# A two-layer sparse graph network on one core: order of the opening work, place of the order scatters, and the engines of the quantile mean

## The chip, the core and the metric

The kernel runs on one core of one Trainium2 chip. A core has a tensor engine (PE, with its weight loads counted apart as PEld), a vector engine (DVE), a scalar engine (ACT), GpSimd (POOL) and a sync engine (SP) that mostly issues transfers. Each engine works through its own list of instructions in order, and waits at an instruction until what it needs is there. The metric is the device time of one execution in microseconds.

## The reference

There are N = 4096 nodes with 128 features, and an adjacency matrix of 4096 x 4096 int32 with about 64 neighbours per node. Cut to what matters:

```python
# layer 0: graph attention, 8 heads
Wh = einsum('nd,hde->hne', nodes, W)
e  = leaky_relu((Wh @ a1)[:, :, None] + (Wh @ a2)[:, None, :])
att = softmax(where(adj > 0, e, -9e15))
h  = elu(einsum('hnm,hmd->hnd', att, Wh))
x1 = layernorm(nodes + elu(cat(h) @ W1 + b1))
# layer 1: mean of three quantiles over the kept neighbours
rank = cumsum(mask) - 1                     # every m-th neighbour is removed
keep = mask & ~((rank + 1) % m == 0)        # m = ceil(number / 2), if number > 5
svals = sort(where(keep, x1[None], big), axis=1)     # per feature
agg = sum(svals[ceil(q * n_keep) - 1] / 3 for q in (0.25, 0.5, 0.75))
out = (0.5 * agg + 0.5 * x1) @ W.T + b + x1
```

## The kernel before

Nodes are handled in 32 tiles of 128, one node per partition. `gnn` (L2138) runs layer 0 in `gat` (L761) and then, on a flag in memory, `sparse` (L1570) for graphs with few neighbours, the way taken here, or `general`, which takes no part in this execution.

**Lists of neighbours.** The class `Front` (L310) turns the adjacency matrix into sorted lists of neighbours, in six blocks of 4, 4, 6, 6, 6 and 6 tiles. `scan` (L360) loads quarters of rows (`a_i`, 512 KB, SP's queue), takes their sign on ACT (L371, L378: `nz`) and packs 16 columns into one number on PE (L380, `ps_words`, two buffers in PSUM). On DVE, `first` (L390) makes keys from the words (L393) and pulls out the largest eight in 13 rounds (`drain8`, L186 and L188: a maximum and a replacement); `second` (L398) unpacks the words in two more levels; `last_` (L736) sorts what was found. When all tiles of a block are through, `place` (L438) computes where each node's row goes (`pos_i`, L509, so that nodes with like counts share a tile), and POOL scatters the rows to memory (`rows_d`, L530). Then `keep` (L559) computes which neighbours layer 1 keeps, and at the end `order` (L619) and `scatter` (L668, 32 scatters of `order_d` on POOL) write the sequence of nodes for layer 1. `pieces` (L693) gives all this as a list of small steps; a call of `advance(n)` emits the next n of them, so the source chooses where between the attention's steps they are written.

**Attention.** `table` (L228) builds in memory `xf_d`, a row per node with its features and its eight terms of the attention: it loads x (`xf`), transposes it on PE (copies `xT_ta` on ACT, L143), multiplies the attention vectors (`abc_ta`) with the weights on DVE, projects on PE (`ps_fa`, L258), copies the result beside x on ACT (L259) and writes four transfers of 1024 rows (L261). All transfers of `table`, and the weight loads after it (L806 to L818), are issued on ACT's queue. For each of 64 half tiles, `load` (L873) then reads the lists back and gathers neighbour rows from `xf_d`, one row per partition and DMA (`nb`, L890, POOL, 2250 in all). DVE and ACT compute the attention's probabilities (L966, L974, L1005), PE sums weighted rows (L1012), and `combine` projects. The main loop (L1111) calls `advance(2)` per half tile.

**Layer 1.** In `sparse`, for each tile POOL gathers the kept neighbours' rows of x1 (`rows`, L1607, 2078 in all; three buffers). `compare` (L1632) is one step of a sorting network: ACT copies the low side to PSUM (`low`, L1645; small ones to SBUF, `low_s`), DVE takes the minimum (L1650) and the maximum (L1651); one-sided steps are L1653 and L1655. Steps of two tiles are interleaved. When a tile's steps are done, `quantile` (L1657) finds the rows that can be a node's quartile: for some late tiles a chain of minima and maxima (`cut`) first; then per quartile a weight (L1684: 1/3 where the position is the node's own, else 0), and DVE multiplies and adds row by row (L1695, L1698) into `agg`. `finish` (L1702), once per four tiles, has PE average with x1 (L1711, L1712), ACT copy (`comT`, L1716), PE apply the layer (L1722 to L1724), ACT copy `o` (L1728) and POOL scatter it (L1732). The parts of `finish` wait in a list, `waiting`, and are slipped into later comparisons: "copy" parts behind the comparison's own ACT copy, "bank" parts for PE in the last bank of the comparison's PSUM tile, ahead of its minimum:

```python
nc.scalar.copy(packed, lows)
if waiting and waiting[0][0] == "copy":
    waiting.pop(0)[1]()
elif waiting and SMALL < k <= PAIRS - FOUR:
    waiting.pop(0)[1](t[:, (PAIRS - FOUR) * D :])
nc.vector.tensor_tensor(lows, packed, highs, op=ALU.min)
nc.vector.tensor_tensor(highs, packed, highs, op=ALU.max)
```

**What sets the order.** The source is written in one sequence, but the framework arranges each engine's list itself, by data dependencies and its own estimates of when operands are ready; `issue_after(i)` binds what is emitted under it behind instruction i. Buffers of a pool bind too: a tile may be written only when the earlier use of its memory is over.

Of the kernel before, what the change touches and what calls it, by code (L numbers as in the profile page):

```python
# [50 lines left out]
P = 128  # L51
N = 4096
D = 128
# [37 lines left out]
FOUR = 4  # L91

# [135 lines left out]
def table(tc, nc, c, x, w, a1, a2, xf_d):  # L228

    with tc.tile_pool(name="ta", bufs=1) as tp, tc.tile_pool(  # L230
        name="ta_ps", bufs=2, space=PSUM
    ) as psum:
        w_sb = tp.tile([P, H, D], F32, name="w_ta")
        nc.scalar.dma_start(out=w_sb, in_=w.rearrange("h d e -> d h e"))
        pad = tp.tile([1, XF], F32, name="pad_x")
        nc.gpsimd.memset(pad, 0.0)
        nc.gpsimd.memset(pad[:, D : D + H], -BIG)
        nc.scalar.dma_start(out=xf_d[0:1, :], in_=pad)
        xf = tp.tile([P, NT, XF], F32, name="xf")
        for i in range(4):  # L240
            nc.scalar.dma_start(
                out=xf[:, ts(i, 8), :D],
                in_=x[ts(i, 1024), :].rearrange("(t p) d -> p t d", p=P),
            )
        xT = tp.tile([P, N], F32, name="xT_ta")
        transpose_all(nc, psum, xT, [xf[:, t, :D] for t in range(NT)], c["idf"])
        wa = tp.tile([P, 2 * H], F32, name="wa_ta")
        for i, a in enumerate((a2, a1)):
            abc = tp.tile([P, H, D], F32, name="abc_ta", bufs=2)
            nc.scalar.dma_start(  # L250
                out=abc.rearrange("p h e -> p (h e)"),
                in_=a.rearrange("h e -> (h e)").partition_broadcast(P),
            )
            nc.vector.tensor_mul(abc, abc, w_sb)
            nc.vector.reduce_sum(wa[:, ts(i, H)], abc, axis=AX.X)
        ps_f = psum.tile([P, NT, 2 * H], F32, name="ps_fa", bufs=1)
        for t in range(NT):
            nc.tensor.matmul(ps_f[:, t, :], xT[:, ts(t, P)], wa, start=True, stop=True)  # L258
        nc.scalar.copy(xf[:, :, D:], ps_f)  # L259
        for i in range(4):  # L260
            nc.scalar.dma_start(  # L261
                out=xf_d[1 + i * 1024 : 1 + (i + 1) * 1024, :].rearrange(
                    "(t p) d -> p t d", p=P
                ),
                in_=xf[:, ts(i, 8), :],
            )
# [43 lines left out]
class Front:  # L310
# [3 lines left out]
    def __init__(self, tc, nc, c, adj, meta_d, ctx):  # L314
# [43 lines left out]
        self.words, self.lists, self.counts = {}, {}, {}  # L358

# [78 lines left out]
    def place(self, b):  # L438
# [70 lines left out]
        nc.vector.tensor_copy(pos_i, pos)  # L509
# [183 lines left out]
    def pieces(self, order_d, flag_d):  # L693
# [10 lines left out]
        for b, n in enumerate(BLOCKS):  # L704
            lists = self.tp.tile([P, max(BLOCKS), C1], F32, name="lists")

            def open_(b=b, lists=lists):
                self.lists[b] = lists

            out.append(("open", open_))  # L710
            at = START[b]
            while at < START[b] + n:
                m = min(BATCH, START[b] + n - at)
                if n % BATCH:
                    m = n // -(-n // BATCH)
                bufs = {}

                def start(bufs=bufs):
                    bufs["k1"] = self.one.tile([P, BATCH, C1], F32, name="k1")
                    bufs["cand"] = self.one.tile([P, BATCH, CAND], F32, name="cand")  # L720

                for j in range(m):

                    def one_(t=at + j, j=j, bufs=bufs, start=start):
                        if j == 0:
                            start()
                        ahead(t)
                        self.first(t, bufs["k1"][:, j, :])

                    out.append((None, one_))  # L730
                out.append(
                    (None, lambda t=at, m=m, bufs=bufs: self.second(t, m, bufs["k1"], bufs["cand"]))
                )
                for j in range(m):

                    def last_(t=at + j, j=j, b=b, bufs=bufs):  # L736
                        to = self.lists[b][:, t - START[b], :]
                        drain8(self.nc, to, bufs["cand"][:, j, :], C1 // 8, -1.0e6)
                        self.nc.vector.tensor_scalar(
                            self.spill[:, t, 4:5], to[:, C1 - 1 :], 0.0, None, op0=ALU.is_ge  # L740
                        )

                    out.append((None, last_))
                at += m
            out.append((b, lambda b=b: self.place(b)))
            if b:
                out.append((None, lambda b=b: self.keep(b - 1)))
# [8 lines left out]
        for t in range(NT):  # L756
            out.append((None, lambda t=t: self.scatter(t, state["pos"], order_d)))
        return out


def gat(tc, nc, c, x, adj, xf_d, meta_d, order_d, flag_d, w, a1, a2, w1, b1, gamma, beta, x1_d):  # L761
# [22 lines left out]
    with ExitStack() as ctx:  # L784
        front = Front(tc, nc, c, adj, meta_d, ctx)
        todo = front.pieces(order_d, flag_d)
# [13 lines left out]
        table(tc, nc, c, x, w, a1, a2, xf_d)  # L800
# [5 lines left out]
        nc.scalar.dma_start(out=w_sb, in_=w.rearrange("h d e -> d h e"))  # L806
        w1_sb = one.tile([P, H, D], F32, name="w1_ga")
        nc.scalar.dma_start(out=w1_sb, in_=w1.rearrange("(h e) o -> e h o", e=D))
        b1_sb = one.tile([P, 1], F32, name="b1_ga")
        nc.scalar.dma_start(out=b1_sb, in_=b1.rearrange("(o k) -> o k", k=1))  # L810
        bc = {}
        for name, src in (("gamma", gamma), ("beta", beta)):
            bc[name] = one.tile([P, D], F32, name=f"{name}_ga")
            nc.scalar.dma_start(out=bc[name], in_=src.partition_broadcast(P))
        for row, value in PADS:
            pad = one.tile([1, D], F32, name="pad", bufs=2)
            nc.vector.memset(pad, value)
            nc.scalar.dma_start(out=x1_d[row : row + 1, :], in_=pad)  # L818
# [292 lines left out]
        for u in range(2 * NT):  # L1111
            t, half = divmod(u, 2)
            if u + 3 < 2 * NT:
                held[u + 3] = load(u + 3)
            if not half and t + 1 < NT:
# [454 lines left out]
def sparse(tc, nc, c, x1_d, meta_d, order_d, w, b, out):  # L1570


    with tc.tile_pool(name="sp1", bufs=1) as one, tc.tile_pool(
# [11 lines left out]
        nc.scalar.mul(half, c["idf"], 0.5)  # L1585
        wT = one.tile([P, D], F32, name="lwT")
# [4 lines left out]
        third = float(np.float32(1.0 / NQ))  # L1591
# [65 lines left out]
        def quantile(t, rows, info, extra, agg):  # L1657

            shift = MIDDLE - HIGH[t] // 2
            for q, (lo, hi) in enumerate(places(t)):  # L1660
                n = hi - lo + 1
                if extra:
                    cut = one.tile([P, 3 * (80 - MAIN) * D], F32, name="cut")
                    grid = view(cut, 0, (extra, n), (1, extra))
                    nc.vector.tensor_tensor(
                        grid,
                        view(rows, lo - extra - 1, (1, n), (1, extra)),
                        view(rows, MAIN, (0, n), (1, extra)),
# [3 lines left out]
                    while m > 1:  # L1672
                        h = m // 2
                        a = view(cut, 0, (extra, n), (1, h))
                        nc.vector.tensor_tensor(
                            a, a, view(cut, m - h, (extra, n), (1, h)), op=ALU.min
                        )
                        m -= h
                    best = view(rows, lo - 1, (1, n))
                    nc.vector.tensor_tensor(best, best, view(cut, 0, (extra, n)), op=ALU.min)  # L1680
                if q == 0:
                    begun = False
                weight = tp.tile([P, 8], F32, name="weight", bufs=4)
                nc.vector.tensor_scalar(  # L1684
                    weight[:, :n],
                    iota_p[:, lo + shift : hi + 1 + shift],
                    info.bitcast(F32)[:, POS + q : POS + q + 1],
                    third,
                    op0=ALU.is_equal,
                    op1=ALU.mult,  # L1690
                )
                for i in range(n):
                    v = view(rows, lo - 1 + i)
                    if not begun:
                        nc.vector.tensor_scalar(agg, v, weight[:, i : i + 1], None, op0=ALU.mult)  # L1695
                        begun = True
                    else:
                        nc.vector.scalar_tensor_tensor(  # L1698
                            agg, v, weight[:, i : i + 1], agg, op0=ALU.mult, op1=ALU.add
                        )  # L1700

        def finish(xs, agg, infos):  # L1702
# [3 lines left out]

            def halves_(ps):
                made["ps"] = ps
                for j in range(m):
                    com = ps[:, ts(j, P)]  # L1710
                    nc.tensor.matmul(com, agg[:, j, :], half, start=True, stop=False)  # L1711
                    nc.tensor.matmul(com, xs[:, j, :], half, start=False, stop=True)  # L1712

            def half_copy():
                made["comT"] = one.tile([P, FOUR * P], F32, name="comT")
                nc.scalar.copy(made["comT"][:, : m * P], made["ps"][:, : m * P])  # L1716

            def layer(ps):
                made["ps"] = ps
                for j in range(m):  # L1720
# [3 lines left out]
                    nc.tensor.matmul(to, made["comT"][:, ts(j, P)], wT, start=False, stop=True)  # L1724
# [14 lines left out]
            return [("bank", halves_), ("copy", half_copy), ("bank", layer), ("copy", layer_copy)]  # L1739
# [3 lines left out]
        def load(t):  # L1743
            rows = three.tile([P, max(HIGH), D], F32, name="rows")
            first, _ = ENDS[t]
            if t == first:
                group[first] = (
                    tp.tile([P, FOUR, D], F32, name="xs"),
                    tp.tile([P, FOUR, D], F32, name="agg"),
# [17 lines left out]
        for t in range(NT + 1):  # L1767
# [9 lines left out]
            if t > 0:  # L1777
                first, n = ENDS[t - 1]
                agg = group[first][1]
                quantile(t - 1, *held.pop(t - 1), plans[t - 1][2], agg[:, t - 1 - first, :])  # L1780
# [411 lines left out]
```

## Time and profile before

| | |
|---|---|
| median of the runs | 7742.63 us (7739.8 to 7743.64, 3 runs) |
| the profiled execution | 7742.94 us |
| its span, first to last instruction | 7741.1 us |
| DVE busy | 5841.9 us (75%) |
| POOL busy | 4386.7 us (57%) |
| ACT busy | 2162.5 us (28%) |
| PE busy | 1051.4 us (14%) |

A profile line names a source line, an engine, an operation and its operands (out<-in), a count, the busy time and the mean duration, and the idle time of the engine just before, with what ended it. "issue" is idle time for which the profile shows no wait. In the page's slices each digit is the busy share in tenths of one fortieth of the span (193.5 us). A line of waits reads: who waited, for whom, microseconds in all, times, and the longest. A window's line gives the stretch, its length, each engine's busy time with the number of instructions, the granted tensor clock, the share of the DMA engines and GB/s.

### The profile page before, as it was taken

The page shows a single profiled execution, that of the slowest core. Times are in us where ns is not written, and L with a number is a line of the kernel's source. Part 1 is how long each engine was busy: PE and PEld are TensorE (multiplying, and loading weights), DVE is VectorE, ACT ScalarE, POOL GpSimd, SP SyncE. Part 2 cuts the span into 40 slices and gives each one's busy share as a digit, 9 for nine tenths or more (in the row PEclk, how much of TensorE's full clock was granted, in tenths as well). Part 3 has the DMA queues.
Part 4 walks back from the last instruction along what each step waited for, and adds up shares of the span by engine and source line. Part 5 has one row for each costly group of instructions (what it writes and reads, how often), then busy time and mean ns, then how long its engine had stood idle before and what let it go on. Part 6 is the DMA issues. An engine that isn't in the chain of part 4 may idle for free. (4 is left out here: it accounts for less than half of the span.)

```text
span 7741.1 us, 30455 instructions
## 1 busy us (share of the span) xinstructions
PE 1051.4 (14%) x5811; PEld 887.8 (11%) x5811; DVE 5841.9 (75%) x9358; ACT 2162.5 (28%) x2127; POOL 4386.7 (57%) x4564
## 2 busy tenths in 40 slices
PE   3233242332232223200000000000000000000000
PEld 1122232222232222100000000000000000000000
DVE  6456465564332222289999999999999999999999
ACT  5021112000000000133333333333333333333332
POOL 0777777777777777575545636354635534554400
PEclk5566666665566666655555555555555555555555
DMA  5232324222222222111111101011101101111100
GB/s 183 67 100 78 97 78 113 64 60 56 47 56 56 56 56 56 41 48 37 35 32 36 42 24 43 27 38 31 45 23 36 36 27 29 37 36 31 31 3 1
DMA packets 222435, 385.05 MB, mean 50 GB/s; under 512 B 121622, under 2 KB 133274, under 8 KB 222234
## 3 DMA queue, kind: packets, MB, share of 16 engines
q0 software_dynamic: 145664, 305.55, 15.4%
q1 hardware_dynamic: 64258, 70.19, 3.0%
q10 hardware_dynamic: 12312, 7.28, 0.3%
q14 instruction: 154, 1.26, 0.1%
q8 instruction: 47, 0.77, 0.0%
HBM read 372.41 MB, written 10.31 MB: 49 GB/s over the span
## 5 line engine op out<-in xcount | busy, mean ns | idle before, releaser
L1607 POOL DMA_INDIRECT rows<-x_d,info x2078 | 2022.4, 973 | 1962.4 <-DVE agg L1698 1272.7
L890 POOL DMA_INDIRECT nb<-xf_d,ids x2250 | 2140.2, 951 | 697.0 <-issue 652.8
L1645 ACT COPY low<-rows 128x2048 f32<-128x2048 f32 (+8 forms) x1022 | 1561.3, 1533 | 2599.7 <-DVE rows L1651 1964.0
L1650 DVE TENSOR_TENSOR rows<-low,rows 128x2048 f32<-128x2048 f32 (+8 forms) x1022 | 1883.1, 1861 | 114.5 <-ACT low L1645 33.8
L1651 DVE TENSOR_TENSOR rows<-low,rows 128x2048 f32<-128x2048 f32 (+8 forms) x1022 | 1881.7, 1860 | 4.7
L966 DVE TENSOR_TENSOR e<-nb,ps_small 128x144 f32<-128x144 f32 (+8 forms) x166 | 43.5, 264 | 1314.1 <-DMA nb<-xf_d,ids 1246.9
L1012 PE MATMUL ps_z<-spread,nb 128*128 128x128 f32 x4500 | 612.1, 304 | 770.2 <-DVE spread L1005 749.0
L1012 PEld LDWEIGHTS ps_z<-spread,nb 128*128 128x128 f32 x4500 | 601.0, 219 | 804.5 <-DVE spread L1005 367.3
L1711 PE MATMUL low<-half_i,agg 128*128 128x128 f32 x64 | 22.2, 451 | 4297.1 <-ACT low L1645 4191.2
L974 ACT ACTIVATE ps_e<-e 128x256 f32<-128x256 f32 (+4 forms) x64 | 26.1, 408 | 1941.1 <-DVE e L966 1856.6
L1711 PEld LDWEIGHTS low<-half_i,agg 128*128 128x128 f32 x64 | 16.9, 325 | 4300.6 <-ACT low L1645 4193.6
L1005 DVE TENSOR_TENSOR spread<-e,ps_small 128x1152 f32<-128x1152 f32 (+4 forms) x312 | 342.9, 1107 | 87.8 <-PE ps_z L1012 85.3
L1732 POOL DMA_INDIRECT out<-o,info x32 | 33.4, 1044 | 383.6 <-ACT o L1728 359.3
L371 ACT ACTIVATE nz<-a_i 128x1024 bf16<-128x1024 int32 x128 | 134.4, 1051 | 229.4 <-DMA a_i<-in_adj 188.5
L1645 ACT COPY low_s<-rows 128x512 f32<-128x512 f32 (+3 forms) x325 | 139.8, 471 | 142.8 <-DVE rows L1650 61.4
L186 DVE MAX8 k<-key 128x8 f32<-128x256 f32 x416 | 165.7, 413 | 0.9
L1650 DVE TENSOR_TENSOR rows<-low_s,rows 128x512 f32<-128x512 f32 (+3 forms) x325 | 158.0, 499 | 2.6 <-ACT low_s L1645 2.1
L1651 DVE TENSOR_TENSOR rows<-low_s,rows 128x512 f32<-128x512 f32 (+3 forms) x325 | 158.7, 499 | 0.3
L188 DVE MATCH_REPLACE8 key<-k,key 128x256 f32<-128x256 f32 x384 | 155.9, 408 | 0.0
L904 DVE TENSOR_TENSOR mine<-me,group 128x64 f32<-128x64 f32 x32 | 6.8, 213 | 196.6 <-DMA me<-xf_d,info 193.5
L380 PE MATMUL ps_words<-nz,pows 128*128 128x512 bf16 (+1 forms) x272 | 109.8, 559 | 291.9 <-ACT nz L378 192.8
L1653 DVE TENSOR_TENSOR rows<-rows 128x256 f32<-128x256 f32 (+8 forms) x245 | 141.4, 579 | 0.2
(227 smaller groups left out, 2584.8 us busy)
## 6 DMA issues: line engine op xcount, KB each, us to landing
a_i<-in_adj SPq DMA_DIRECT2D x128, 512.0 KB, 4.4
nb<-xf_d,ids POOLq DMA_INDIRECT x2250, 2.5
rows<-x_d,info POOLq DMA_INDIRECT x2078, 2.4
xf_d<-xf ACTq DMA_DIRECT2D x4, 576.0 KB
xf<-in_x ACTq DMA_DIRECT2D x4, 512.0 KB
meta_d<-rowdata_k SPq DMA_DIRECT2D x4, 324.0 KB, 4.0
abc_ta<-in_L_gnn_a ACTq DMA_DIRECT2D x2, 512.0 KB, 8.6
w_ga<-in_L_gnn_W ACTq DMA_DIRECT2D x2, 512.0 KB, 4.9
```

The lines of the kernel that those rows point to most:

```text
L186: nc.vector.max(out=top, in_=work)
L188: nc.vector.match_replace(out=work, in_to_replace=top, in_values=work, imm_value=gone)
L371: nc.scalar.activation(nz[:, j, :], a_i, AF.Relu, scale=-1.0, accum_out=self.negative[:, k : k + 1],)
L380: nc.tensor.matmul(ps_w[:, :m, :], self.pows[:, 4 * i + b, :], nz[:, :m, ts(b, NG1)], start=i + b == 0, stop=i + b == 6,)
L890: gather = nc.gpsimd.indirect_dma_start(out=rows[:, at + i, :], out_offset=None, in_=xf_d, in_offset=bass.IndirectOffsetOnAxis(ap=ids[:, k ...
L1005: last = nc.vector.tensor_tensor(spread[:, :m], e[:, at : at + m, :].unsqueeze(2).to_broadcast(shape), own.unsqueeze(1).unsqueeze(3).to_br ...
L1012: product = nc.tensor.matmul(ps_z[:, g, :], rows[:, k + i0 + i, :D], spread[:, i].rearrange("p j h -> p (j h)"), start=i0 + i == 0, stop=i ...
L1607: nc.gpsimd.indirect_dma_start(out=row, out_offset=None, in_=x1_d, in_offset=bass.IndirectOffsetOnAxis(ap=info[:, col : col + 1], axis=0),)
L1645: nc.scalar.copy(packed, lows)
L1650: nc.vector.tensor_tensor(lows, packed, highs, op=ALU.min)
L1651: nc.vector.tensor_tensor(highs, packed, highs, op=ALU.max)
L1653: nc.vector.tensor_tensor(lows, lows, highs, op=ALU.min)
```

## The change

It has three parts. (A) The transfers of `table` and the weight loads go to POOL's queue; the scans of block 0 are emitted within `table` (`between`), ahead of the transposes; and `first` of the later blocks may be issued only behind block 0's `pos_i`. (B) The 32 order scatters are taken out of the list of pieces and emitted once no further half tile is left to load. (C) The quantile mean no longer runs on DVE: DVE makes one weight (1 or 0) for all three quartiles of a tile, ACT multiplies each found row by it (`picked`), and PE adds the rows and x1 by products with scaled identities (`sixth`, `half`), per tile; ACT copies the sum. The chain of minima and maxima is done in pieces of at most 32 rows.

```diff
-def table(tc, nc, c, x, w, a1, a2, xf_d):
+def table(tc, nc, c, x, w, a1, a2, xf_d, between):
...
-        nc.scalar.dma_start(out=w_sb, in_=w.rearrange("h d e -> d h e"))
+        nc.gpsimd.dma_start(out=w_sb, in_=w.rearrange("h d e -> d h e"))
...
+        for a in (a2, a1):
+            abc = tp.tile([P, H, D], F32, name="abc_ta", bufs=2)
+            nc.gpsimd.dma_start(
...
         for i in range(4):
-            nc.scalar.dma_start(
+            nc.gpsimd.dma_start(
                 out=xf[:, ts(i, 8), :D],
...
+        between()
+        for i, abc in enumerate(abcs):
+            nc.vector.tensor_mul(abc, abc, w_sb)
+            nc.vector.reduce_sum(wa[:, ts(i, H)], abc, axis=AX.X)
...
         for i in range(4):
-            nc.scalar.dma_start(
+            nc.gpsimd.dma_start(
                 out=xf_d[1 + i * 1024 : 1 + (i + 1) * 1024, :].rearrange(
...
-        nc.vector.tensor_copy(pos_i, pos)
+        placed = nc.vector.tensor_copy(pos_i, pos)
+        if b == 0:
+            self.placed = placed.ins
...
-                        self.first(t, bufs["k1"][:, j, :])
+                        with ExitStack() as order:
+                            if self.placed is not None:
+                                order.enter_context(self.tc.issue_after(self.placed))
+                            self.first(t, bufs["k1"][:, j, :])
...
-        for t in range(NT):
-            out.append((None, lambda t=t: self.scatter(t, state["pos"], order_d)))
-        return out
+        late = [lambda t=t: self.scatter(t, state["pos"], order_d) for t in range(NT)]
+        return out, late
...
         advance(1)
-        table(tc, nc, c, x, w, a1, a2, xf_d)
+        table(tc, nc, c, x, w, a1, a2, xf_d, lambda: advance(2))
...
-        nc.scalar.dma_start(out=w_sb, in_=w.rearrange("h d e -> d h e"))
+        nc.gpsimd.dma_start(out=w_sb, in_=w.rearrange("h d e -> d h e"))
...
                 held[u + 3] = load(u + 3)
+            elif late:
+                advance(len(todo))
+                for piece in late:
+                    piece()
+                late = []
...
+        sixth = one.tile([P, P], F32, name="sixth_i")
+        nc.scalar.mul(sixth, c["idf"], 0.5 * float(np.float32(1.0 / NQ)))
...
+            nc.vector.tensor_tensor(
+                weight[:, :, : last - first + 1],
+                iota_p[:, first + shift : last + 1 + shift].unsqueeze(1).to_broadcast(shape),
+                info.bitcast(F32)[:, POS : POS + NQ].unsqueeze(2).to_broadcast(shape),
+                op=ALU.is_equal,
+            )
...
                 for i in range(n):
-                    v = view(rows, lo - 1 + i)
-                    if not begun:
-                        nc.vector.tensor_scalar(agg, v, weight[:, i : i + 1], None, op0=ALU.mult)
-                        begun = True
-                    else:
-                        nc.vector.scalar_tensor_tensor(
-                            agg, v, weight[:, i : i + 1], agg, op0=ALU.mult, op1=ALU.add
-                        )
+                    at = lo - first + i
+                    found.append((view(rows, lo - 1 + i), weight[:, q, at : at + 1]))
+            return found
+
+        def pick(found, x1, comT):
+            made = {}
+            def scale():
+                made["v"] = tp.tile([P, MOST, D], F32, name="picked", bufs=1)
+                for i, (v, weight) in enumerate(found):
+                    nc.scalar.mul(made["v"][:, i, :], v, weight)
+            def sums(ps):
+                made["ps"] = ps[:, :P]
+                for i in range(len(found)):
+                    nc.tensor.matmul(
+                        made["ps"], made["v"][:, i, :], sixth, start=i == 0, stop=False
+                    )
+                nc.tensor.matmul(made["ps"], x1, half, start=False, stop=True)
+            return [
+                ("copy", scale),
+                ("bank", sums),
+                ("copy", lambda: nc.scalar.copy(comT, made["ps"])),
+            ]
...
-            return [("bank", halves_), ("copy", half_copy), ("bank", layer), ("copy", layer_copy)]
+            return [("bank", layer), ("copy", layer_copy)]
...
+                found = quantile(t - 1, *held.pop(t - 1), plans[t - 1][2])
+                waiting += pick(found, xs[:, at, :], comT[:, at, :])
```

## The prediction

> **What bounds the kernel now.** The slices of the page come first: they show stages with different limits. In slice 0 POOL does nothing; to about slice 16 it is the busy engine; from slice 17 VectorE (DVE) is at nine tenths.
>
> ```profile
> DVE  6456465564332222289999999999999999999999
> ACT  5021112000000000133333333333333333333332
> POOL 0777777777777777575545636354635534554400
> ```
>
> Cut at the stages, busy time per engine (columns: PE, PE weight loads, DVE, ACT, POOL) says how full each is.
>
> ```profile
> 0.00:170.50 170.50, 58.37 (x194) 32.77 (x194) 114.75 (x595) 102.28 (x160) 1.59 (x11) 0.57 0.58 187
> 170.50:3189.00 3018.50, 872.82 (x5154) 758.93 (x5154) 1342.87 (x5088) 345.14 (x578) 2260.52 (x2374) 0.63 0.28 69
> 3245.00:7741.10 4496.10, 94.53 (x320) 74.34 (x320) 4354.56 (x3599) 1702.05 (x1365) 2120.43 (x2174) 0.50 0.11 32
> ```
>
> In the first stage no engine is full: it is a chain that ends at DVE's `pos_i`, for which POOL waits 166.6 us. In the second, POOL goes from gather to gather, 951 ns and 0.30 us of issue, 1.25 us each, while DVE waits 1246.9 us for `nb`. In the third DVE has 4354.6 of 4496.1 us, so a microsecond of DVE work there is a microsecond of time. Groups of the page and of the third stage:
>
> ```profile
> L890 POOL DMA_INDIRECT nb<-xf_d,ids x2250 | 2140.2, 951 | 697.0 <-issue 652.8
> ...
> L1698 DVE SCALAR_TENSOR_TENSOR agg<-rows,weight,agg 128x128 f32<-128x128 f32 x118 | 40.2, 341 | 0.8
> ...
> L1645 ACT COPY low_s<-rows 128x128 f32<-128x128 f32 x57 | 16.3, 294 | 12.3 <-DVE rows L1655 5.8 <-DVE rows L1650 4.2 <-DVE rows L1651 1.8
> ```
>
> The waits of the first 200 us tell what delays `pos_i`:
>
> ```profile
> POOL rows_d L530 <- DVE pos_i L509: 166.6, 1, 166.6
> ...
> DVE pad L817 <- DMA xf_d<-xf: 22.0, 1, 22.0
> ...
> ACT xf L259 <- PE ps_fa L258: 14.7, 1, 14.7
> ...
> ACT nz L378 <- DMA w_ga<-in_L_gnn_W: 10.2, 1, 10.2
> ...
> ACT nz L378 <- issue: 4.1, 1, 4.1
> ```
>
> ACT stands still three times (14.7, 4.1 and 10.2 us) in the table's copy and DMA issues, with adjacency scans queued behind; DVE then gets the words of tiles 2 and 3 at 87.9 us.
>
> **Part A: first block ahead of the table.** Nineteen DMAs leave ACT's queue for POOL's; block 0's scans stand before the table, and DVE's first-level searches of later blocks are held behind block 0's `pos_i`.
>
> The ACT side: sixteen quarter-row scans are all that tiles 0 to 3 need, 2.31 us each (four took 9.22 us from 78.88). From a start near 6 us: 6 + 16 x 2.31 + 3.3 (`pows`) + 8 x 0.53 (`xT` copies) = 50.5, and about 3.5 for late loads and the last words on PE: words of the pair at about 54 us (50 to 60) instead of 87.4.
>
> The DVE side: after 7 of the 13 rounds of the pair's search stands a memset that waits until the `xf_d` writes have landed (the same wait is the 22.0 us of L817 now). DVE is there at about 66. The copy into `xf` follows the seventeenth scan on ACT, at about 59. Now the writes go out on ACT, 48.43 us, and are down at 61.6, 13.1 later. On POOL no row shows a plain DMA of 1024 rows. The nearest are indirect ones: 0.95 us for 128 descriptors. From below, one plain DMA costs as much as one of those (landed about 72, DVE not held long); from above, eight times as much, 7.6 us (landed about 92). Neither is nearer; I take the middle, 4.3: landed 79, so a wait of 13 us stays.
>
> Then, with durations of the trace: 0.9 (memset and small ones) + 8.6 (six rounds left) + 13.5 (second level) + 28 (last level, 27.9 now) + 11.5 (placing, with `keep` between) = 62.5; `pos_i` at 141.5 instead of 170.1. What drops out on the way is 17.8 us of later blocks' key work, which comes after `pos_i` and fills DVE's waits for gathers (about 104 us idle between 200 and 400). From `pos_i` to the first gather is 9.85 us now (170.08 to 179.93), kept: 151.4 against 179.9, **-28.5**. POOL's issue carries this through the second stage one to one, if no later block's `pos_i` is late: block 1 has it at 369.7 for a scatter at 432.9, block 4 at 1524.1 for one at 1540.3. DVE had waited for gathers before each, so these times move with POOL. Ends: -36 by the low price, -16 by the high one, -12 with late words too.
>
> A rule speaks against this part. The Trainium skill, "DMA: Bandwidth & Descriptors", section "SWDGE vs HWDGE vs iDMA", gives plain transfers to SP or ACT, because GpSimd builds descriptors in software. By the rule alone A loses: the landing goes from 61.6 to 79 or 92. By the rows it wins: ACT's three stalls, 29 us, are on the path, POOL is idle 166.6 us, and the later landing runs into a DVE that is itself busy until 66. I follow the rows for the sign, and the rule for the 13 us that stay.
>
> **Part B: order scatters last.** The 32 scatters of `order_d` (1965.8 to 2081 us, 32 x 1.25 = 40 us of POOL) are written after the last gather in the source. But in the compiled order of POOL's instructions they stand among the gathers as before: 13 behind the last block's rows, then 6, 8, 4, 1, with some 180 gathers still to come. No instruction moves, so **0**; if they did move, into POOL's idle time at the end of the stage, -40.
>
> **Part C: quantile mean.** Removed from DVE: L1698 118 times (40.2 us), and by rows of the same view L1695 32 times (8.8) and L1684 96 times (20.1): 69.1 us busy. Records overlap by 0.07 us, as here (start, duration):
>
> ```profile
> 7719.01 0.28 DVE L1653 TENSOR_TENSOR rows<-rows 128x128 f32<-128x128 f32 x1
> 7719.22 0.74 DVE L1655 TENSOR_TENSOR rows<-rows 128x256 f32<-128x256 f32 x2
> ```
>
> 69.1 - 246 x 0.07 = 51.9. Added: 32 weight comparisons at the 277 ns of a 128x128 operation, 0.21 net each, 6.6; six more cut operations in one tile, 1.2. DVE: **-44**. The last tile's 13 (4.99 us) give way to 14 scales and 15 matmuls at the very end, 4 to 7 us: no gain there, within 2 either way.
>
> ACT gets 150 scales of 128x128. No row has a scale by a per-partition pointer; nearest are the plain copy at 294 ns and `yT`, whose bias pointer costs 55 ns over its twin without (471 against 416). About 0.30 us net each, 4.7 per tile: 1.4 us. ACT is 38% busy there and mostly waits for DVE, but DVE now waits 33.8 us in 43 places for ACT's copy, so the lead is short at times: estimated a quarter of a microsecond per tile, **+8** (0 to 45).
>
> PE gets 3 to 7 matmuls per tile (15 for tiles 0 and 31) in place of 8 per four tiles. They use the last bank of a `low` tile, and the minimum behind waits:
>
> ```profile
> DVE rows L1650 <- ACT low L1645: 33.8, 43, 1.9
> ...
> DVE rows L1650 <- PE low L1724: 22.1, 7, 5.5
> ...
> DVE rows L1650 <- PE low L1712: 2.5, 4, 1.3
> ```
>
> The twelve matmuls of the layer stall DVE 3.2 us a time, the eight of the halves 0.6. Five (0.43 each, 2.2 us) should nearly hide: 0.2 x 32 = **+6** (0 to 70), less the 2.5 of the halves. POOL's gathers wait for the freeing of `rows` with at least 22 us to spare. C: -44 - 2.5 + 6 + 8 = **-32.5** (-46 to +69 with both ends at once).
>
> Here a rule bears too: "ScalarE: Activation LUTs", section "Rules for kernel authors", puts multiplication on VectorE, not ScalarE. Per operation that agrees with the trace (277 against 294 ns). By the rule the move costs 150 x 0.02 = 3 us; by the stage rows it frees 44, since DVE is full and ACT idle.
>
> **Sum.** -28.5 + 0 - 32.5 = -61 on the profiled 7742.94 (span 7741.1, 1.8 around it). The median of the runs shown is 7742.63, 0.3 lower: 7742.6 - 61 = 7681.6, said as **7680**. What a measurement can tell is 0.2%, 15.5 us.
>
> **Rivals.** (1) A turns into a wait for POOL's descriptors: x and the weights also go through POOL, so `xf` itself is late, and DVE stands at the pad memset till 92 or beyond. For: no plain DMA on POOL in the trace, the rule above. Against: POOL has nothing else. A gives -16 to 0: 7694 to 7710. (2) C is eaten, ending on the other side. In a comparison with a sum, ACT copy, PE matmuls and DVE minimum stand in a row; if scales (1.4) and sums (2.2) both show fully, 3.6 x 32 = 115, C is +69; with A: 7742.6 - 28.5 + 69 = 7783. For: the layer's 3.2 us. Against: the halves' 0.6. It is slower from 2.3 us per tile on, (28.5 + 46.5) / 32. (3) C is half eaten, 1.1 us per tile (35), -11: 7703. (4) B happens after all: 7640. A and C both leading to nothing is left among (2) and (3).
>
> **How the numbers follow.** Likeliest (A and C as summed) 0.57, own range 7660 to 7697; rival 1 0.20; rival 3 0.13; rival 4 0.06; rival 2 0.04. The range reaches from 7648 (low price for A, C unhindered, without B) to 7716 (rivals 1 and 3 in part together), leaving out some 0.2. Faster by over 0.2% means below 7727: all but rival 2 and a sliver of 1 with 3, 0.93; same 0.03; slower 0.04.
>
> **What would show it.** A: `pos_i` near 141 and first gather near 151; DVE's pad wait 5 to 26 us; no ACT stall on `w_ga`; words of tiles 2 and 3 near 54. B: order scatters still between 1900 and 2100. C: DVE busy in the third stage 44 lower; waits of L1650's successor for ACT under 45, for PE under 32. Wrong: `pos_i` after 155, a wait for `pos_i` at a later block, or PE and ACT waits of over 60 together.

## The result

The changed kernel takes 7694.65 us (median of 4 runs, 7692.66 to 7695.29), the kernel before 7741.75 (7739.8 to 7743.64): a ratio of 0.9939, 95% interval 0.9922 to 0.9956, or 47 us less. The prediction was 7680, 62 us less, with a range of 7648 to 7716. The profiled execution has a span of 7693.5 us against 7741.1, 47.6 us less. Some runs below, marked as paused, were taken while the chip added pauses, mostly of 10 to 45 us, to every kernel, so that the kernel before took 8506 or 8553 us; their times are compared only with those of the kernel before taken beside them, and otherwise their traces are read by their waits.

Of the changed kernel, the windows of the front up to `pos_i` and the first gather, the stage of gathers, the passage to layer 1, layer 1, and the end (stretch, length, busy time of PE, PE weight loads, DVE, ACT, POOL):

```profile
132.60:142.30 9.70, 4.81 (x12) 1.64 (x13) 9.70 (x42) 6.18 (x9) 3.96 (x5) 0.68 0.23 35
142.30:3151.00 3008.70, 878.83 (x5158) 761.93 (x5157) 1351.37 (x5102) 356.18 (x593) 2256.00 (x2370) 0.62 0.28 71
3151.00:3230.90 79.90, 25.24 (x143) 21.42 (x143) 30.22 (x81) 14.19 (x26) 22.80 (x25) 0.67 0.08 22
3230.90:7676.30 4445.40, 148.66 (x524) 119.92 (x524) 4316.19 (x3389) 1751.38 (x1527) 2106.12 (x2154) 0.50 0.11 32
7676.30:7693.50 17.20, 7.93 (x34) 6.92 (x33) 0.01 (x1) 3.20 (x12) 0.96 (x1) 0.60 0.01 4
```

The same stretches of the kernel before, cut at the same points (the last cut is the end of DVE's last instruction, a maximum now and a product of the quantile mean before):

```profile
170.10:179.90 9.80, 3.20 (x8) 1.11 (x9) 9.80 (x43) 1.28 (x3) 3.98 (x4) 0.52 0.25 35
179.90:3189.30 3009.40, 869.62 (x5147) 757.82 (x5145) 1333.47 (x5049) 343.85 (x576) 2256.53 (x2370) 0.63 0.28 70
3189.30:3269.30 80.00, 25.68 (x143) 21.73 (x143) 30.41 (x82) 13.87 (x25) 22.41 (x25) 0.67 0.08 21
3269.30:7727.00 4457.70, 91.46 (x310) 71.98 (x310) 4353.84 (x3595) 1700.72 (x1362) 2101.18 (x2154) 0.50 0.11 32
7727.00:7741.10 14.10, 3.07 (x10) 2.36 (x10) 0.00 (x0) 0.53 (x2) 0.97 (x1) 0.50 0.02 5
```

The front is 37.6 us shorter (first gather at 142.3 instead of 179.9), the stage of gathers and the passage to layer 1 keep their length to a microsecond, and layer 1 with its end goes from 4471.8 to 4462.6, 9.2 less (4462.0 in `b_real_2` below, which has the same layer 1). So part A gave 38.4 us by the first minimum of layer 1 and part C 9.2. The order scatters lie between 1934.8 and 2042.9 us, inside the stage of gathers as before: part B did nothing.

What the front waits for now:

```profile
POOL rows_d L541 <- DVE pos_i L518: 56.7, 1, 56.7
...
POOL w_ga L819 <- DMA xf_d<-xf: 11.0, 1, 11.0
...
DVE pad L830 <- ACT nz L380: 7.0, 1, 7.0
...
ACT xf L267 <- PE ps_fa L266: 3.2, 1, 3.2
```

ACT's three stalls, 29 us together, have shrunk to one of 3.2. DVE's wait in front of the pad is 7.0 us instead of 22.0. The view names an ACT instruction as its releaser, but POOL's `w_ga`, which waits for the same memory, is released by `xf_d` in the same instant (72.0 us). POOL's own timeline has the transfers:

```profile
57.45 3.56 POOL L269 DMA_DIRECT2D xf_d<-xf  x4 [48.21 <-ACT xf L267]
72.01 0.89 POOL L819 DMA_DIRECT2D w_ga<-in_L_gnn_W  x1 [11.00 <-DMA xf_d<-xf]
...
133.10 1.04 POOL L541 DMA_INDIRECT rows_d<-rowdata,pos_i  x1 [56.72 <-DVE pos_i L518]
...
142.29 0.98 POOL L903 DMA_INDIRECT nb<-xf_d,ids  x1 [4.32 <-DMA ids<-rows_d]
```

A plain transfer of 1024 rows costs POOL 0.89 us (four in 3.56). From the start of the first (57.45) to the pad (71.86) it is 14.4 us.

In layer 1, the waits of DVE from the first minimum on:

```profile
DVE rows L1670 <- ACT low L1665: 49.7, 51, 1.9
DVE rows L1670 <- DMA rows<-x_d,info: 30.2, 2, 20.5
DVE rows L1670 <- PE low L1751: 20.2, 8, 3.3
DVE rows L1670 <- DMA xs<-x_d,info: 14.4, 1, 14.4
DVE rows L1670 <- PE low L1732: 12.6, 11, 2.2
```

ACT's copies cost DVE 49.7 us (33.8 before), PE's layer and sums 32.8 (layer and halves before: 22.1 + 2.5 = 24.6). DVE's work fell by 37.7 (4353.84 to 4316.19), and 24 of it came back as these waits; the end of the last tile, counted from DVE's last instruction, took 3.1 us more (17.2 instead of 14.1).

### The profile page after: what moved, and what is told of

Read it like the earlier page. It is cut to its first block, busy times and chain, and to the rows that moved or that the text cites. A ratio compares the mean times of both kernels' runs of the same rounds, so it can differ in the third digit from the quotient of the medians.

```text
span 7693.5 us, 30931 instructions
## 1 busy us (share of the span) xinstructions
PE 1110.2 (14%) x6047; PEld 938.3 (12%) x6047; DVE 5809.0 (76%) x9150; ACT 2215.2 (29%) x2301; POOL 4405.6 (57%) x4583
## 5 line engine op out<-in xcount | busy, mean ns | idle before, releaser
L1670 DVE TENSOR_TENSOR rows<-low,rows 128x2048 f32<-128x2048 f32 (+9 forms) x1022 | 1884.7, 1862 | 139.0 <-ACT low L1665 49.7
L1671 DVE TENSOR_TENSOR rows<-low,rows 128x2048 f32<-128x2048 f32 (+9 forms) x1022 | 1882.4, 1861 | 5.8
L1729 PE MATMUL low<-sixth_i,picked 128*128 128x128 f32 x300 | 80.4, 445 | 4224.2 <-ACT low L1665 3735.9
L1729 PEld LDWEIGHTS low<-sixth_i,picked 128*128 128x128 f32 x300 | 67.3, 327 | 4237.2 <-ACT low L1665 3744.4
L380 ACT ACTIVATE nz<-a_i 128x1024 bf16<-128x1024 int32 x128 | 134.4, 1051 | 236.8 <-DMA a_i<-in_adj 213.6
L1056 PE MATMUL ps_h<-zT,w_ga 128*128 128x256 f32 x256 | 111.5, 599 | 205.4 <-DVE s L1328 105.1
```

The source lines that it names most:

```text
L380: nc.scalar.activation(nz[:, j, :], a_i, AF.Relu, scale=-1.0, accum_out=self.negative[:, k : k + 1],)
L1729: nc.tensor.matmul(made["ps"], made["v"][:, i, :], sixth, start=i == 0, stop=False)
```

## The experiments

**Each part alone.** Part C alone is the change to `sparse` laid on the kernel before; part A alone is the change to `table`, the loads and the hold behind `pos_i`.

```diff
-                quantile(t - 1, *held.pop(t - 1), plans[t - 1][2], agg[:, t - 1 - first, :])
+                found = quantile(t - 1, *held.pop(t - 1), plans[t - 1][2])
+                waiting += pick(found, xs[:, at, :], comT[:, at, :])
```

> The kernel before with part C alone (A and B undone). Theory: C is worth little on its own account, as the changed trace reads: DVE work -38 us, DVE waits +25 us, end of the last tile +3 us, so -10 us: 7732 (7728 to 7736). Rival: C is worth the -32 us of the prediction and A loses a part of its gain later: 7710.

Measured, paused: 8511.95 us against 8506.15 of the kernel before, ratio 1.0011 (1.0003 to 1.0018). Both numbers missed: under pauses C alone was slower by 6 us. The traces say where. From the first minimum of layer 1 to the end of DVE's last instruction, without waits of over 3.5 us (most of them pauses), `c_only` takes 4437.7 us, and `a_only` and `order_only`, which have layer 1 as before and were taken beside it, take 4437.7 both: under pauses the waits, short pauses among them, ate all of C's 38 us, where undisturbed they ate 24. The end behind it is 17.7 us against 12.1 and 13.8. C alone was not measured undisturbed; its size there, 9.2 us, is that of layer 1 in the traces of the kernels before and after.

```diff
-        table(tc, nc, c, x, w, a1, a2, xf_d)
+        table(tc, nc, c, x, w, a1, a2, xf_d, lambda: advance(2))
...
+                            if self.placed is not None:
+                                order.enter_context(self.tc.issue_after(self.placed))
```

> The kernel before with part A alone. Theory: first gather near 142 us, and the 38 us gained there stay to the end: 7704 (7701 to 7707). Rival (A given back in layer 1, C worth -32): 7725. Last gather of neighbours 38 us earlier than before in both.

Measured beside it: 8453.66 us, ratio 0.9939 (0.9917 to 0.9961), 52 us less than the kernel before, with pauses in it. Its `pos_i` is at 132.9 us and the first gather at 142.8, as in the changed kernel (132.6 and 142.3); those of `c_only` are at 170.4 and 180.2. So A makes the front's gain by itself. That it gives nothing back is seen in the undisturbed traces: gather for gather, the changed kernel stays 35.0 to 40.4 us ahead from the first to the last of the 2250.

**Order or queue?** Part A with all ten transfer statements of `table` and the loads put back on ACT's queue:

```diff
-            nc.gpsimd.dma_start(
+            nc.scalar.dma_start(
                 out=xf[:, ts(i, 8), :D],
```

> Part A's order alone: block 0's scans within the table and the hold behind pos_i, with all transfers left on ACT's queue; no B, no C. Theory (the order carries most of A, the queue little): pos_i at 134 to 143 us, some 27 to 36 us earlier than before, time near 7710. Rival (ACT's queue is what delayed the front): pos_i later than 155 us, time above 7725.

`pos_i` came at 135.7 us: 34.4 of the 37.5 us are the order (block 0's scans first, later searches behind `pos_i`), and some 3 the queue. The queue's share is the less sure one: in nine traces with the changed order and POOL's queue `pos_i` lies between 130.0 and 132.9, so it is 3 to 6. The time, one paused run of 8493.7, says no more than that it is below 8506. The words of tiles 2 and 3 are there at 61.4 us, 8 later than in the changed kernel, but ACT's four transfers need only 11.7 us from the first start (63.5) to the landing, and the pad's wait is 1.9 us, its releaser named:

```profile
75.21 0.31 DVE L829 MEMSET pad<- 1x128 f32 x2 [1.92 <-DMA xf_d<-xf]
```

**Part B made real.** One binding more, so that the scatters cannot be drawn ahead of the gathers:

```diff
+                with ExitStack() as order:
+                    order.enter_context(tc.issue_after(gathers[2 * NT - 1][-1]))
                     for piece in late:
-                    piece()
+                        piece()
```

> The changed kernel, with the 32 order scatters bound behind the last gather of neighbours, so that part B happens. Theory: B has moved nothing so far; POOL's 40 us leave the stage that its gathers bound and fall into the 40 us in which POOL waits for the last tile: 38 to 40 us faster than the changed kernel, 7655. Rival: the last rows of layer 0 or the reading back of the sequence queue behind them, and the first gather of layer 1 is no earlier: 7695; half of it: 7675.

Paused it took 8453.86, ratio 0.9944 (0.9925 to 0.9963), no better than A alone. The trace shows the scatters in their new place, and a pause of DVE of 29.35 us right behind them, so it decides nothing. Undisturbed:

> The same kernel as b_real (order scatters bound behind the last gather of neighbours), again, because the chip of the first time added pauses of tens of microseconds to all kernels, the kernel before too. Against a kernel before of 7742: theory 7655 (40 us less than the changed kernel: last gather near 3110, first gather of layer 1 near 3173); rival 7695 (the last rows of layer 0 queue behind the scatters).

7657.5 us against 7744.39, ratio 0.9888 (0.9872 to 0.9905): 37 us less than the changed kernel, as the theory says. POOL's timeline at the passage (the 32 scatters stand between the last gather and the first line below; the last of them starts at 3151.78):

```profile
3111.34 0.94 POOL L903 DMA_INDIRECT nb<-xf_d,ids  x1 [0.30 <-issue]
...
3153.04 0.95 POOL L1111 DMA_INDIRECT x_d<-s,info  x1 [0.30 <-issue]
...
3175.16 0.95 POOL L1629 DMA_INDIRECT xs<-x_d,info  x1 [0.30 <-issue]
```

The last gather starts 38.4 us earlier than in the changed kernel (3149.8), and the first of layer 1 37.6 earlier (3212.8); 1.5 of this were there at the first gather (the front varies that much from trace to trace). The scatters fill the 40.06 us in which POOL waited for the last tile. The next `x_d` scatter follows with 0.30 us between, so the rival's queue begins just there.

**Where C's gain went.** Two kernels leave work out. In the first, ACT scales only a tile's first found row; in the second, PE adds only the first scaled row and x1.

```diff
-                for i, (v, weight) in enumerate(found):
+                for i, (v, weight) in enumerate(found[:1]):
                     nc.scalar.mul(made["v"][:, i, :], v, weight)
...
-                        made["ps"], made["v"][:, i, :], sixth, start=i == 0, stop=False
+                        made["ps"], made["v"][:, 0, :], sixth, start=i == 0, stop=False
```

> The changed kernel, but ACT multiplies only the first found row of a tile by its weight, and PE adds that row as often as there were rows (32 scales in place of 150; the mean is left out in this form). Theory (the scales on ACT cost DVE some 16 us of waits for ACT's copies): 7679 (7675 to 7685), DVE's waits for ACT's copies back near 34 us. Rival (the waits come with PE's sums or the copies of them): 7690 to 7696.

```diff
-                for i in range(len(found)):
+                for i in range(1):
                     nc.tensor.matmul(
```

> The changed kernel, but PE adds only the first scaled row and x1 (2 matmuls per tile in place of 5.7; the other rows are left out of the sum). Theory (PE's sums cost DVE some 8 to 13 us of waits): 7685 (7681 to 7689), waits for the sums gone. Rival (the scales carry the waits, the sums nothing): 7692 to 7696.

Both, a second time (all four are paused):

> The kernel of one_scale again (ACT scales one row per tile, PE adds it as often as before), since pauses of the chip covered its first run. Against a changed kernel of 7694.7. Theory (scales cost DVE 16 us or more, as the 20 us between the paused runs suggest): 7675 to 7680, waits for ACT's copies back to 30 to 35 us. Rival (no part of the missing gain is theirs): 7692 to 7696.

> The kernel of two_sums again (PE adds one scaled row and x1 per tile), since pauses of the chip covered its first run. Against a changed kernel of 7694.7. Theory as now revised (sums hold the PSUM buffer that ACT's next copy but one needs, so they cost in both waits, 20 us or more): 7670 to 7675, waits for ACT's copies below 35 us, waits for the sums near 0. First theory (only DVE's own waits for the sums, 8 to 13 us): 7682 to 7687.

First time (kernel before 8553.49): 8491.58, ratio 0.994 (0.9918 to 0.9962), and 8465.21, ratio 0.9905 (0.9882 to 0.9927). Second time (8505.61): 8435.27, ratio 0.9918 (0.9899 to 0.9938), and 8420.16, ratio 0.9904 (0.9884 to 0.9924). None of the numbers expected against 7694.7 can be held to these. What can be compared is layer 1 counted as above, from its first minimum to the end of DVE's last instruction without waits of over 3.5 us. The changed kernel's program for layer 1 was in three paused traces (`c_only`, `b_real`, `pad_apart`):

| layer 1 without waits over 3.5 us | us |
|---|---|
| the program before, two traces | 4437.7, 4437.7 |
| the changed kernel's program, three traces | 4437.7, 4437.1, 4439.3 |
| one scale per tile, two traces | 4418.9, 4426.2 |
| two sums per tile, two traces | 4406.1, 4407.4 |

So under pauses the scales cost 11 to 20 us, near the 16 expected, and the sums 30 to 33, far more than the 8 to 13 of the first theory. Pauses of under 3.5 us are still in all of these (34 to 37 us in the changed program's traces, 34 and 45 with one scale, 30 with two sums), so each size is good to some 5 us. The waits say why. With `pad_apart` as the changed kernel's program:

```profile
DVE rows L1670 <- ACT low L1665: 43.1, 42, 2.1
...
DVE rows L1670 <- PE low L1732: 10.2, 8, 2.5
```

and in the second trace of two sums:

```profile
DVE rows L1670 <- remote: 126.8, 5, 37.6
DVE rows L1670 <- issue: 45.6, 20, 22.4
DVE rows L1670 <- ACT low L1665: 28.6, 32, 1.9
```

where the waits for PE's sums are gone, and those for ACT's copies have fallen from 43.1 to 28.6, though ACT still does all 150 scales. ("remote" and "issue" are the pauses. This view begins 37 us into layer 1; counted from its first minimum it is 30.4, and 29.3 in the first trace.) With one scale per tile the waits for ACT's copies are 31.3 and 33.0. PE's work thus shows in ACT's copies too. That this is by the PSUM buffer, which stays taken until the sum is copied out while only two take turns, fits the code but was not tried by itself. These sizes are those under pauses, where C added 38 us of waits; how the 24 of the undisturbed kernel divide between scales and sums was not tried.

**Is it a matter of place?** The same work, but a scale or a sum is slipped in only where a running count of both engines' time shows DVE to be far enough behind:

```diff
-                if waiting and waiting[0][0] == "copy":
-                    waiting.pop(0)[1]()
+                elif kind == "scale" and fits(kind, size, k, end, 10):
+                    waiting.pop(0)
+                    part()
...
+        def fits(kind, size, k, end, limit):
+            lead["age"] += 1
+            late = lead["age"] / limit
+            if kind == "scale":
+                room = max(lead["dve"], end) + 0.12 + 0.27 * k - end - 1.8
+                return room >= (0.1 + 0.3 * size) * (1 - late)
+            return lead["dve"] - end >= (0.3 + 0.45 * size) * (1 - late)
```

> The changed kernel with the same work, but a scale or a sum is slipped in only where a running count of ACT's and DVE's time says that DVE has enough work ahead (at the latest ten to twelve comparisons later). Theory (the waits are a matter of place): 12 to 20 us of the 25 come back, 7678. Rival (there is no room in the comparisons, the waits move only): 7690 to 7700.

Measured beside the first two above: 8459.84, ratio 0.9894 (0.9871 to 0.9917). Without the long waits layer 1 has 4429.7 us, 7 to 10 less than the three traces of the changed program: less than the theory, more than the rival. But the end behind DVE's last instruction takes 23.8 us, against 16.6 to 17.7 in the three, so little of it reached the end of the kernel.

**DVE's wait for the table's memory.** The pad, group, place and wide tiles are taken from a pool of the front, so they no longer lie where `xf` was:

```diff
-            pad = one.tile([1, D], F32, name="pad", bufs=2)
+            pad = front.one.tile([1, D], F32, name="pad", bufs=2)
```

> The changed kernel with the pad, group, place and wide tiles in a pool of the front, so that DVE need not wait in the middle of block 0's search for the transfers into xf_d. Theory (the 7.0 us of that wait are on the path to pos_i and go to the end one to one): pos_i near 125.6, 7688. Rival (something else of the table holds DVE or the first gather): pos_i unchanged or the first gather late, 7693 to 7696.

Measured beside it: 8526.49, ratio 0.9969 (0.9961 to 0.9977), a time that the pauses rule. `pos_i` is at 125.1 us, 7.5 before the changed kernel's, and the first gather at 134.9, 7.4 before. The nine traces with the wait (5.1 to 7.1 us) have `pos_i` at 130.0 to 132.9, the two without it at 125.1 and 124.6: the wait was on the path, one to one as far as this spread can tell.

**All three together.**

> The changed kernel with three mends together: the order scatters bound behind the last gather, the pad, group, place and wide tiles in a pool of the front, and scales and sums slipped in by the running count. On a chip where the kernel before takes 7742: theory (they add: 7657 of the bound scatters, 7.5 less from the front, 10 to 15 less from the placing) 7637 (7632 to 7643). Rival (the placing only moves the waits): 7650. DVE's waits in layer 1 for ACT's copies below 38 us and for PE's sums and layer below 20 us by the theory, 50 and 33 by the rival.

7644.93 us (7644.14 to 7647.18) against 7744.85, ratio 0.9871 (0.9855 to 0.9888), undisturbed: 50 us below the changed kernel, the fastest of all. It lies between theory (7637) and rival (7650), above the theory's range and nearer the rival. First gather at 134.4, last at 3104.0, so front and scatters add up in full: 45.8 us earlier than in the changed kernel. Layer 1 from its first minimum to the end took 4455.9 us against 4462.0 of `b_real_2`, 6 less where 10 to 15 were expected. Cut at DVE's last instruction, `all_three` first, then `b_real_2`:

```profile
3186.40:7618.60 4432.20, 139.43 (x502) 113.25 (x502) 4314.80 (x3389) 1749.48 (x1522) 2091.73 (x2151) 0.50 0.13 32
7618.60:7642.30 23.70, 12.44 (x54) 10.69 (x54) 0.00 (x0) 4.63 (x15) 3.88 (x4) 0.64 0.03 11
...
3193.40:7638.40 4445.00, 148.28 (x524) 119.55 (x524) 4316.17 (x3389) 1751.29 (x1527) 2106.58 (x2154) 0.50 0.13 32
7638.40:7655.40 17.00, 7.71 (x34) 6.80 (x33) 0.04 (x1) 3.23 (x12) 0.96 (x1) 0.60 0.01 4
```

So the placing did give 12.8 us, as expected, up to DVE's last instruction, and 6.7 were lost behind it: the parts held back so long are still undone when DVE ends, and PE applies the layer to three more tiles (7618.7 to 7624.3) before the last tile's sums. DVE's waits in layer 1:

```profile
DVE rows L1701 <- ACT low L1676: 46.8, 55, 1.9
...
DVE rows L1701 <- PE low L1782: 17.4, 7, 3.9
...
DVE rows L1701 <- PE low L1763: 6.9, 5, 1.4
```

The waits for sums halved (12.6 to 6.9) and those for the layer fell by 3; the waits for ACT hardly moved (46.8, where below 38 was expected; sums and layer 24.3, where below 20). The simple count places PE's work better than ACT's.

## Why the prediction was right, and where it was not

*Sum and sign.* Faster, and inside the range; the forecast of -61 became -47, by an A that was too small by 9 and a C that was too large by 23. The two errors have opposite signs, and that the sum came as near as 15 us is luck: with A as forecast and C as measured it would have been 7705, in the stated range but outside the likeliest one (7660 to 7697).

*A, the ACT side.* Right: the words of tiles 2 and 3 were there at 53.3 us (54 forecast), DVE stood at the pad memset at 64.8 (66).

*A, the landing.* Mis-sized: the landing of `xf_d`. The middle of the two bounds, 4.3 us per plain transfer on POOL, was taken since neither row was nearer; it measured 0.89, just under the lower bound, and the writes were down at 72.0, where the lower bound had put them, though in another way: they began 1.5 us before the forecast's 59 and took over 14 us instead of 13. So DVE waited 7.0 and not 13 us. The rest of the chain took 60.6 us (72.0 to 132.6) against 62.5, and with 9.7 us to the first gather A was -37.6 instead of -28.5.

*A, the rule.* The rule of the Trainium skill ("DMA: Bandwidth & Descriptors", section "SWDGE vs HWDGE vs iDMA") that gives plain transfers to SP or ACT was a reason to expect 13 us of wait. The four transfers occupied POOL for less time than ACT (3.56 us against 5.02 before), but they landed later: from the first start to the pad it is 14.0 to 14.5 us in the nine traces with POOL's queue, 11.7 to 13.2 in the three with ACT's (`before`, `c_only`, `order_only`). So the rule has the right direction here, with 1 to 3 us, if other traffic has no part in it; and it costs less than keeping ACT free brings: with the same order but ACT's queue, `pos_i` was 3 us later, not earlier.

*A, one to one.* Right: no block's `pos_i` was late, and the 37.6 us of the first gather were still there (38.4) at the first minimum of layer 1.

*B.* Right: no scatter moved, and no time came of it. The rival's size (-40) is right too, as 37 us in `b_real_2` show. Two readings were off without harm: the scatters began at 1973.4 us, not 1965.8, and behind them 866 gathers were still to come, not 180. (In part A, 104 us between 200 and 400 us was DVE's busy time; idle were 96.)

*C, DVE's work.* Nearly right: -37.7 against -44. What went and what came in measured as forecast (53 and 7 us against 52 and 8); but the minima and maxima, in the same numbers, took 8 us more than before (4182 to 4190, each counted to the start of the next, without the wait between). A wait ahead of an instruction ends its overlap with the one before, but at 0.07 us a time that explains only a part, and the rest was not followed.

*C, the waits.* This is the step that failed, in size. Forecast were +8 for ACT's scales and +6 less 2.5 for PE's sums, 11.5 together; ACT's copies cost 15.9 more (33.8 to 49.7) and PE 8.2 more (24.6 to 32.8), 24.1 together, about twice as much in both terms. The single prices were right: twelve scales took 3.61 us in the last tile, 0.29 us each (0.30 forecast), and twelve sums 5.49, 0.46 each (0.43). What failed is the step from price to wait. The sums were judged by the halves, eight matmuls that cost DVE 0.6 us in each of 4 places; the sums cost it 12.6 us in 11 places, 1.1 each, and there are 32 of them where there were 9 groups of halves. And ACT's waits were priced by the scales alone; the paused traces show that leaving out the sums lowers them as much as leaving out the scales does (to 29 to 31 and 31 to 33 us, from 40 to 45). This second effect the forecast left out.

*C, the rule.* The advice of the Trainium skill ("ScalarE: Activation LUTs", section "Rules for kernel authors") to keep multiplication on VectorE was set aside because DVE was full. DVE did get 37.7 us shorter; but 24 of them were handed back, so following the advice would have cost 9 us here and not 44.

*The end.* Within the 2 us forecast: from the last maximum to the end 19.0 us before (7722.1 to 7741.1), 17.2 now.

*Signs.* Those for A and B came as stated, `pos_i` and the first gather 9 us early. Of those for C, DVE's work was 38 lower instead of 44, the waits for ACT were 49.7 (under 45 was asked) and for PE 32.8 (under 32). Together they are 82.5, over the 60 that was to show the prediction wrong; that sign was badly set, since the forecast itself came to 70 (58.4 before and 11.5 more), but it did point at the step that failed.

*Rivals.* Rival 1 (POOL's descriptors as the new bound) is refuted by the 0.89 us and by the landing at 72.0. Rival 3 (C half eaten) is what happened to C, somewhat worse: -9 rather than -11. Rival 2 needed 2.3 us of waits per tile to make the kernel slower; 24.1 over 32 tiles are 0.75.

## What to carry to other kernels

Work moved off the full engine is worth what it weighs less what the full engine then waits for the engines that took it over. Price that wait at every engine that stands in line behind the moved work, not only at the first: here the sums on PE also lengthened the waits for ACT. Work held back for a better place has to be done before the full engine ends, or it lengthens the end. Where a framework arranges the queues, writing a step later may move nothing, as here: look at the arranged order, and bind the step behind something if it has to stay behind. At the head of a program, look for the one result that starts the bounding stage and put nothing ahead of it that it does not need, waits for reused memory included.

## What the runs showed of the hardware that was not expected

A plain transfer of 1024 rows of 576 bytes occupies POOL no longer (0.89 us) than a gather of 128 rows (0.94 to 0.98).

Under the pauses PE, ACT and DVE stood still together for tens of microseconds while POOL went on for most of it. In `c_only`, for example (columns as above):

```profile
4928.00:4966.00 38.00, 0.00 (x0) 0.00 (x0) 0.00 (x0) 0.00 (x0) 23.64 (x25) 0.50 0.17 43
```

The pauses are bound to places of the program: in `c_only`, `b_real` and `pad_apart`, whose layer 1 is the same and begins between 3788 and 3844 us, the seven long ones stand before the same DVE instructions (the 467th from the first minimum, the 815th, the 1171st and so on), the first 626 to 629 us into layer 1. In `placed`, which arranges the same work differently, the first long one comes after 322 us. One chip showed the pauses at one time and not at another. Their cause stays open.
